# Second attention of a conv-attention network: projections in a written order, values made turned, statistics in PSUM, a scale per slot

## The chip, the cores and the metric

The kernel runs on one core of one Trainium2 chip. It is one launch that computes a whole network of four layers. The metric is the device time of an execution in microseconds (us). Three timed runs of the kernel before gave 3449.45, 3446.09 and 3445.12 us, a median of 3446.09.

The core has engines with instruction queues of their own: TensorE (PE in the profile; PEld is its loading of weights), VectorE (DVE), ScalarE (ACT), GpSimd (POOL) and SyncE (SP). They work side by side and wait for each other by semaphores. SBUF is the memory that all of them read; PSUM is the memory that TensorE writes its products to, in banks of 2 KB for each of 128 partitions.

## The reference, cut to what matters

The input is one image of 256 channels and 64x64 points, so 4096 tokens of width 256. The changed part is the attention of the third layer ("L2"). Its reference, after a layer norm of x and cut to the operations (H = 8 heads of h = 32):

```
q, k, v = linear(x) each, as (B, H, L, h)
sim = sum_d(q * k) * qk_norm_scale
k = l2_normalize(k);  v = l2_normalize(v)
Z = einsum('bhld,bhle->bhlde', v, k) * kv_norm_scale
gates = square(relu(Z.reshape(B, H, L, h*h) @ wg_w.T + wg_b)) + EPS
m_scan, s_scan = online softmax scan of sim along L
Z_scan = cumsum(gates * Z, axis=L);  g_scan = cumsum(gates, axis=L)
softmax_weights = exp(sim - m_scan) / (s_scan + EPS)
attn_weights = Z_scan / (g_scan + EPS) * (1 + silu(softmax_weights))
out = linear(einsum('bhld,bhlde->bhle', q, attn_weights))
```

The result is added to the residual. A mixture of experts follows: layer norm, a router, the two best of eight experts for each token.

## The kernel before, in words

The residual `t` lies in SBUF as 32 tiles of 128 tokens by 256 channels. `attn2` (L1375) goes through it in three stages.

**Projections** (`attn2_project`, L1465; called from L1402). The unit is a block of 4 tiles, 512 tokens; there are 8. For a block, `norm` makes the layer norm (`layer_norm`, in parts by `norm_parts`, L201: statistics on DVE, `root` as an add of eps on DVE, L217, and a square root on ACT, L218, then reciprocal and shift on DVE and the application `a_n` on ACT, L232). `turn` transposes it on PE into channels by tokens (`to_channels`, L238). `project(i)` makes q, k and v of a tile as rows (tokens by channels): two products into PSUM, 512 columns for q and k, 256 for v, and a DVE add of the bias for each (L1492). `turn_v` transposes the values to `vT`. `lengths` squares v and k on ACT (L1499), sums the squares per head on DVE (L1500), multiplies q by k on POOL (L1502) and makes 1/(|v||k|) (L1503 to L1507). `sims` sums the products of q and k (L1511). `gates` mixes `vT` by the gate's weights `wg_bd` on PE, multiplies by k (L1524), sums per head (L1526), and turns the sums into gates (L1527 to L1532), by which POOL multiplies the keys (L1533).

Only PE's order is written by hand here (the loop at L1405 to L1414). The order on DVE, ACT and POOL is made by a scheduler. `to_channels` takes PSUM under the tag "a"; the products of `project` take the tag "b" with four buffers, the mixes the tag "u".

**Factors** (`attn2_fac`, L1560). Sums of the gates and the softmax of sim run along all tokens, so they are scans. The 32 tiles' values are turned so that a partition holds a segment (a segment of 256 tokens of a head), scanned within the segment on DVE, and carried across segments by `carry` (L1592): the segments' ends go through PE to 8 partitions (`a_c`), a short scan runs there, and a second product brings the carry back (`a_back`). This happens twice, for sums and maxima and then for the softmax's total. In between, `beside(n)` issues the next n of 31 state products (`attn2_states`, L1539): the outer products of keys and values of a tile, copied from PSUM by ACT in groups of four tiles (L1554) and summed up along the tiles on POOL (L1556). All four engines' order is written here. At the end stand the reciprocals (L1645, L1648), the Silu (L1647) and the transposed factor, which is copied to `fac` (L1654).

**Sum** (`attn2_sum`, L1656). The unit is a slot `u` of 2 tiles; there are 16. `scale(u)` multiplies q by its factor on POOL (L1671), `bias(u)` adds the output's bias to `t` on POOL (L1674), `turn` transposes q, `scores` makes v times q within the tile and masks it on DVE (L1695), `context` adds what earlier tiles' states give (L1706) to what the tile itself gives (L1712) and scales the sum on ACT (L1725), and `out` projects it (`a_o_ps`) and adds it to `t` (L1731). All four engines' order is written: all scales and biases stand ahead of the loop, and in the loop the router's work of the expert layer (`route`, whose layer norm comes from `norm_parts` too) is woven between the slots.

Of the kernel before, what the change touches and what calls it, by code (L numbers as in the profile page):

```python
# [19 lines left out]
P = 128  # L20
C = 256
# [37 lines left out]
for _name, _n in [  # L59
    ("bout0", 2), ("dw_w", 18), ("dw_b", 2), ("ln_g", 2), ("ln_b", 2), ("b_out", 2), ("bn_g", 2), ("bn_b", 2), ("bn_mean", 2),  # L60
    ("bn_var", 2), ("bq3", 2), ("bk3", 2),
]:
    PP[_name] = slice(_at, _at + _n)
    _at += _n
# [24 lines left out]
class Net:  # L89
# [6 lines left out]
    def constants(self, pool):  # L96
        nc = self.nc
        self.ident = pool.tile([P, P], F32, tag="ident", name="ident")
        make_identity(nc, self.ident)
        self.ones_row = pool.tile([1, P], F32, tag="ones_row", name="ones_row")  # L100
        nc.gpsimd.memset(self.ones_row, 1.0)
        self.one = pool.tile([P, 1], F32, tag="one", name="one")
        nc.gpsimd.memset(self.one, 1.0)
        self.ones_col = self.one

        self.flags = pool.tile([P, 3], F32, tag="flags", name="flags")
        self.mom = pool.tile([P, 2, 2], F32, tag="mom", name="mom")

        self.grp = pool.tile([P, 16, 8], F32, tag="grp", name="grp")
        nc.gpsimd.memset(self.grp, 0.125)  # L110
        nc.gpsimd.affine_select(out=self.grp, in_=self.grp, pattern=[[-8, 16], [0, 8]], base=0,
                                channel_multiplier=1, compare_op=ALU.is_ge, fill=0.0)
        nc.gpsimd.affine_select(out=self.grp, in_=self.grp, pattern=[[8, 16], [0, 8]], base=7,
                                channel_multiplier=-1, compare_op=ALU.is_ge, fill=0.0)
        self.pp = pool.tile([P, NPP], F32, tag="pp", name="pp")
        nc.sync.dma_start(out=self.pp, in_=self.A["pp"])
# [84 lines left out]
    def norm_parts(self, pool, x, out, eps, on_act):  # L201
# [13 lines left out]
        def root():  # L215
            r = got["r"] = room("ln_rstd")
            nc.vector.tensor_scalar_add(r, mv[:, :, 1], eps)  # L217
            nc.scalar.activation(r, r, AF.Sqrt)  # L218
# [1156 lines left out]
    def attn2(self, t, S):  # L1375

        nc, tc = self.nc, self.tc
        with tc.tile_pool(name="a2", bufs=1) as pool:
# [16 lines left out]
            with (  # L1395
                tc.tile_pool(name="a2w", bufs=2) as wp,
                tc.tile_pool(name="a2_ps", bufs=2, space=PSUM) as ps,
            ):
                self.rows(wp, "b_qkv2", "b_qkv2")


                stages = [self.attn2_project(b, t, A, wg_bd, wp, ps) for b in range(NBLK)]  # L1402
                go = lambda b, *names: [stages[b][nm]() for nm in names if 0 <= b < NBLK]
                with tc.manual_schedule(engines={mybir.EngineType.PE}):
                    go(0, "norm", "turn")  # L1405
                    for b in range(-1, NBLK):
                        go(b + 2, "norm")
                        go(b + 1, 0)
                        go(b, "turn_v", "lengths")
                        go(b + 1, 1, 2)  # L1410
                        go(b, "sims")
                        go(b + 1, 3)
                        go(b + 2, "turn")
                        go(b, "gates")  # L1414
# [50 lines left out]
    def attn2_project(self, b, t, A, wg_bd, wp, ps):  # L1465


        nc, w = self.nc, self.w
        tiles = slice(b * TPB, (b + 1) * TPB)
        pairs = slice(2 * b, 2 * b + 2)  # L1470
        heads = lambda x: x.rearrange("p t (h d) -> p t h d", d=D)
        of = lambda nm: A[nm].rearrange("p a s h -> p s a h")[:, pairs]
        by_tile = lambda x: x.rearrange("p (s a) h -> p s a h", a=2)
        q, k, v = A["qk"][:, tiles, 0:C], A["qk"][:, tiles, C:], A["v"][:, tiles, :]
        vT = A["vT"][:, :, b * NB : (b + 1) * NB]
        room = lambda: wp.tile([P, TPB, C], F32, tag="room", name="a2_room", bufs=3)
        held = {}

        def norm():
            held["n"] = wp.tile([P, TPB, C], F32, tag="n", name="a2_n", bufs=1)  # L1480
            self.layer_norm(wp, t[:, tiles, :], held["n"], 1e-5, on_act=True)

        def turn():
            held["nT"] = wp.tile([P, 2, NB], F32, tag="nT", name="a2_nT", bufs=1)
            self.to_channels(ps, "a", held["n"], held["nT"], on_act=True)

        def project(i):
            ti, nT = b * TPB + i, held["nT"]
            for dst, lo, hi in ((A["qk"][:, ti, :], 0, 2 * C), (A["v"][:, ti, :], 2 * C, 3 * C)):
                p = ps.tile([P, hi - lo], F32, tag="b", name="a2_qkv_ps", bufs=4)  # L1490
                self.mm(p, [(nT[:, kt, i * P : (i + 1) * P], w["w_qkv2"][:, kt, lo:hi]) for kt in range(2)])
                nc.vector.tensor_add(dst, p, self.row("b_qkv2")[:, lo:hi])  # L1492

        def lengths():

            ss = wp.tile([P, 2, TPB, NH], F32, tag="ss", name="a2_ss")
            for j, x in ((1, v), (0, k)):
                sq = room()
                nc.scalar.activation(sq, x, AF.Square)  # L1499
                nc.vector.tensor_reduce(ss[:, j], heads(sq), AX.X, ALU.add)  # L1500
            held["tmp"] = room()
            nc.gpsimd.tensor_tensor(held["tmp"], q, k, ALU.mult)  # L1502
            nc.vector.tensor_scalar_max(ss, ss, 1e-24)  # L1503
            nc.scalar.activation(ss, ss, AF.Sqrt)
            held["r"] = wp.tile([P, TPB, NH], F32, tag="r", name="a2_r")
            nc.vector.tensor_mul(held["r"], ss[:, 0], ss[:, 1])
            nc.vector.reciprocal(held["r"], held["r"])  # L1507

        def sims():
            sim = wp.tile([P, TPB, NH], F32, tag="sim", name="a2_simt")  # L1510
            nc.vector.tensor_reduce(sim, heads(held["tmp"]), AX.X, ALU.add)  # L1511
            nc.vector.tensor_tensor(of("sim"), by_tile(sim), bc(bc(self.row("qk_scale"), 1, 2), 1, 2), ALU.mult)

        def turn_v():
            self.to_channels(ps, "a", v, vT, on_act=True)

        def gates():
            u = room()
            for i in range(0, TPB, 2):
                p = ps.tile([P, 2, 2, P], F32, tag="u", name="a2_u_ps")  # L1520
                for j in range(2):
                    for m in range(2):
                        self.mm(p[:, j, m, :], [(vT[:, m, (i + j) * P : (i + j + 1) * P], wg_bd[:, m, :])])
                nc.vector.tensor_mul(u[:, i : i + 2, :], p.rearrange("p t m c -> p t (m c)"), k[:, i : i + 2, :])  # L1524
            g = wp.tile([P, TPB, NH], F32, tag="g", name="a2_g")
            nc.vector.tensor_reduce(g, heads(u), AX.X, ALU.add)  # L1526
            nc.vector.tensor_mul(g, g, held["r"])  # L1527
            nc.vector.tensor_scalar(g, g, self.row("wg_b"), 0.0, ALU.add, ALU.max)
            nc.vector.tensor_mul(g, g, g)
            nc.vector.tensor_scalar_add(g, g, 1e-5)  # L1530
            nc.scalar.copy(of("gate"), by_tile(g))
            nc.vector.tensor_mul(g, g, held["r"])  # L1532
            nc.gpsimd.tensor_tensor(heads(k), heads(k), bc(g, 3, D), ALU.mult)  # L1533

        call = lambda i: lambda: project(i)
        return {"norm": norm, "turn": turn, "lengths": lengths, "sims": sims, "turn_v": turn_v, "gates": gates,
                **{i: call(i) for i in range(TPB)}}

# [21 lines left out]
    def attn2_fac(self, A):  # L1560
# [5 lines left out]
        with (  # L1566
# [25 lines left out]
            def carry(ends, scan, first, fill):  # L1592
# [5 lines left out]
                beside(fill)  # L1598
                self.mm(p.rearrange("p j s -> p (j s)"), [(hot, R.rearrange("p j s -> p (j s)"))])
                c = pool.tile([NH, len(ends), NS], F32, tag="c", name="a2_c")  # L1600
# [6 lines left out]
                beside(1)  # L1607
                self.mm(p, [(hotT, x[:, :, 0:NS])])
                z = pool.tile([P, len(first), NS], F32, tag="z", name="a2_z")
# [10 lines left out]
            def sums_and_tops(x, c):  # L1620
# [16 lines left out]
            nc.vector.tensor_scalar_add(gs, gs, 1e-5)  # L1637
            tot = pool.tile([P, L], F32, tag="tot", name="a2_tot")
# [3 lines left out]
                       (0.0,), 12)  # L1642
# [5 lines left out]
            nc.vector.reciprocal(gs, gs)  # L1648
            nc.vector.scalar_tensor_tensor(s, s, 1.0, gs, ALU.add, ALU.mult)
            beside(len(states))  # L1650
# [5 lines left out]
    def attn2_sum(self, t, A, tri, ked, wp, ps, route):  # L1656
# [15 lines left out]

        def bias(u):
            nc.gpsimd.tensor_tensor(t[:, two(u), :], t[:, two(u), :], bc(self.row("wo_b"), 1, 2), ALU.add)  # L1674
# [66 lines left out]
        with self.tc.manual_schedule(engines={ET.PE, ET.DVE, ET.Activation, ET.Pool}):  # L1741
            scale(0)
            scale(1)
            bias(0)
            turn(0)
            scores(0)
            for u in range(2, U):
                scale(u)
                bias(u - 1)
            bias(U - 1)  # L1750
            for u in range(U + 6):
                if u + 1 < U:
# [1085 lines left out]
def lay_out(i):  # L2838
# [44 lines left out]
        "bq3": cols(i["L3_attn_bq"]), "bk3": cols(i["L3_attn_bk"]),  # L2883
# [30 lines left out]
```

## Time and profile before

| what | us |
|---|---|
| median of three runs | 3446.09 |
| the profiled execution | 3443.01 |
| its span, first to last instruction | 3441.5 |
| projections, first product to `a_rows` | 1445.64 to 1568.44 |
| factors, to the first `scale` | 1568.44 to 1590.69 |
| sum with the router, to about | 1750 |
| PE busy over the span | 3103.2 (90%) |
| DVE, POOL, ACT busy | 2311.1, 1457.5, 1327.2 |

The mean clock that TensorE was granted over the execution was 0.951 of full speed.

How to read the lines of the profile that follow. A line of the timeline gives the start in us from the span's begin, the duration, the engine, the line of the program, the operation, what it writes and reads, the shapes, and a count where several in a row are put together; in brackets stands how long the engine was idle before, and which engine, tile and line ended that wait. A matmul in 32-bit floats is two instructions. A line of the windows gives a stretch, its length, and the busy time and number of instructions of each engine in it, then the granted clock, the busy share of the DMA engines and GB/s.

### The profile page before, as it was taken

The numbers are of one execution on the slowest core, as the hardware profiler recorded it, in microseconds if no ns is written. First come the engines' busy times: TensorE is split into PE (matmuls) and PEld (weight loads), VectorE is DVE, ScalarE is ACT, GpSimd is POOL, SyncE is SP. The second block draws the span as 40 slices with busy tenths as digits, with TensorE's granted clock in tenths as the row PEclk, the third lists the DMA queues.
The fourth block names the chain that finished last, engine by engine and source line by source line (L and its number), as shares of the span: only waits on it lengthen the run. The fifth ranks groups of instructions, "written<-read, shape, count | busy, mean of one in ns | idle before, by whom it ended". The sixth has DMA issues, their size and how long they took to land.

```text
span 3441.5 us, 66218 instructions
## 1 busy us (share of the span) xinstructions
PE 3103.2 (90%) x25772; PEld 2319.7 (67%) x25772; DVE 2311.1 (67%) x5339; ACT 1327.2 (39%) x2554; POOL 1457.5 (42%) x1323
## 2 busy tenths in 40 slices
PE   6779999999977899896969789999999996999997
PEld 3443444344436888665857567888888885999996
DVE  8885777577754677796855576777777775555552
ACT  4444334444425666242633352222222222333331
POOL 2028788778843555326344352000000003555552
PEclk9889999999988999897979899999999997999998
DMA  2146556521134222100158643323333214555554
GB/s 74 40 114 142 161 154 168 130 68 52 48 116 111 68 74 73 44 1 2 52 183 264 215 181 127 98 86 98 99 99 98 91 64 154 200 194 199 206 206 176
DMA packets 241688, 407.01 MB, mean 118 GB/s; under 512 B 78353, under 2 KB 152850, under 8 KB 231890
## 3 DMA queue, kind: packets, MB, share of 16 engines
q1 hardware_dynamic: 212002, 344.40, 32.2%
q0 software_dynamic: 13056, 35.93, 2.8%
q10 hardware_dynamic: 16304, 22.31, 1.9%
q8 instruction: 207, 3.39, 0.4%
q14 instruction: 119, 0.97, 0.1%
HBM read 287.07 MB, written 111.30 MB: 116 GB/s over the span
## 4 chain that ended last, share of the span: by engine, by line
PE 42%; DVE 9%; DMA 5%; issue 5%; ACT 3%; POOL 3%; SPq 0%; POOLq 0%; DVEq 0%; ACTq 0%
PE a_sa_ps L2537 6%; PE f_h_ps L146 5%; DMA ys<-f_y,f_at 3%; PE l_acc_ps L1154 3%; PE a_oa_ps L2576 3%; PE a_ob_ps L2576 3%; PE a_oc_ps L2576 3%; PE a_sb_ps L2537 3%; PE f_ya_ps L146 2%; PE f_yb_ps L146 2%; POOL ys L2292 2%; DVE l_pr L1150 2%; PE a_od_ps L2576 1%; PE a_q_ps L146 1%; PE a_qkv_ps L146 1%
## 5 line engine op out<-in xcount | busy, mean ns | idle before, releaser
L770 ACT COPY l_sc<-l_s 128x384 f32<-128x384 f32 (+1 forms) x632 | 304.0, 532 | 456.9 <-PE l_s L763 445.0
L775 DVE TENSOR_TENSOR l_sm<-l_s,mask 128x256 f32<-128x256 f32 (+2 forms) x628 | 308.2, 552 | 89.2 <-PE l_s L763 88.0
L2103 POOL DMA_INDIRECT xs<-f_room,f_to x64 | 64.5, 1007 | 698.0 <-issue 582.4
L146 PE MATMUL f_h_ps<-f_xT,f_w 128*128 128x256 f32 x1440 | 341.1, 388 | 19.4 <-DVE f_xT L2212 9.7
L146 PEld LDWEIGHTS f_h_ps<-f_xT,f_w 128*128 128x128 f32 x1440 | 262.2, 192 | 84.0 <-ACT f_h L2222 31.3
L763 PE MATMUL l_s<-l_q,l_k 32*128 32x256 f32 (+3 forms) x2944 | 270.5, 453 | 0.0
L2556 ACT ACTIVATE a_e<-a_e 128x512 f32<-128x512 f32 x256 | 156.0, 629 | 246.2 <-DVE a_e L2526 245.2
L780 POOL TENSOR_TENSOR l_sm<-l_sc,mask 128x768 f32<-128x768 f32 (+1 forms) x116 | 201.9, 1748 | 88.2 <-ACT l_sc L770 88.1
L2222 ACT ACTIVATE f_h<-f_h_ps,f_w 128x256 f32<-128x256 f32 x360 | 166.6, 470 | 187.9 <-PE f_h_ps L146 178.7
L1150 DVE TENSOR_TENSOR l_pr<-l_vk,l_w_ps 128x1280 f32<-128x1280 f32 x128 | 186.7, 1482 | 55.2 <-PE l_acc_ps L1154 37.6
L763 PEld LDWEIGHTS l_s<-l_q,l_k 32*128 32x128 f32 x2944 | 132.4, 183 | 115.2 <-issue 67.5
L2292 POOL DMA_INDIRECT ys<-f_y,f_at x144 | 145.7, 1012 | 140.6 <-ACT f_y L2291 110.0
L1154 PE MATMUL l_acc_ps<-ident,l_pr 128*128 128x128 f32 x1600 | 198.1, 278 | 7.7 <-POOL l_pr L1145 7.6
L1154 PEld LDWEIGHTS l_acc_ps<-ident,l_pr 128*128 128x128 f32 x1600 | 184.7, 144 | 14.1 <-POOL l_pr L1145 8.3
L784 POOL TENSOR_TENSOR l_sm<-l_sc,mask 128x256 f32<-128x256 f32 (+1 forms) x220 | 184.9, 868 | 16.1 <-ACT l_sc L770 15.2
L2249 POOL TENSOR_TENSOR f_wt<-f_w 128x512 f32<-128x512 f32 x72 | 89.8, 1268 | 217.1 <-PE f_ya_ps L146 204.9
L2537 PE MATMUL a_sa_ps<-a_q,a_kt 128*128 128x256 f32 x512 | 155.6, 386 | 15.1 <-DVE a_u L2542 14.3
L2541 ACT COPY a_u<-a_sa_ps 128x256 f32<-128x256 f32 x128 | 47.6, 372 | 292.0 <-PE a_sa_ps L2537 292.0
L809 PE MATMUL l_b_ps<-l_sm,l_v 128*32 128x256 f32 (+2 forms) x2176 | 153.7, 372 | 0.0
L2537 PE MATMUL a_sa_ps<-a_qt,a_kt 128*128 128x256 f32 x512 | 152.3, 379 | 0.0
L780 POOL TENSOR_TENSOR l_sm<-l_sc,mask_c 128x768 f32<-128x768 f32 (+1 forms) x64 | 122.9, 1937 | 39.7 <-ACT l_sc L770 39.2
L2537 PE MATMUL a_sb_ps<-a_qt,a_kt 128*128 128x256 f32 x512 | 131.4, 379 | 0.0
(558 smaller groups left out, 7292.1 us busy)
## 6 DMA issues: line engine op xcount, KB each, us to landing
a_kt<-a_kd SPq DMA_DIRECT2D x128, 512.0 KB
f_w<-in_f_w SPq DMA_DIRECT2D x36, 1152.0 KB
f_w<-in_f_w SPq DMA_DIRECT2D x36, 1028.0 KB
xs<-zero SPq DMA_DIRECT2D x8, 4160.0 KB
l_vk<-vt SPq DMA_DIRECT2D x180, 128.0 KB
f_x<-xs SPq DMA_DIRECT2D x72, 260.0 KB
f_w<-in_f_w SPq DMA_DIRECT2D x36, 384.0 KB
l_rcp<-l_recd SPq DMA_DIRECT2D x48, 256.0 KB
```

The source lines that it names most:

```text
L146: self.nc.tensor.matmul(out, lhsT, rhs, start=(i == 0), stop=(i == len(pairs) - 1))
L763: nc.tensor.matmul(s[pair, j][:, at : at + m, :], key(hp), qs[hp], start=(z == 0), stop=(z == len(pieces) - 1))
L770: nc.scalar.copy(sc[:, j], s[1, j])
L775: nc.vector.tensor_tensor(to(pair, j, kind, at), pick(s[pair, j], kind, which), mask, ALU.mult)
L780: nc.gpsimd.tensor_tensor(out[:, :, at, :], of[:, :, which, :], bc(mask, 1, 2), ALU.mult)
L784: nc.gpsimd.tensor_tensor(to(1, j, kind, at), pick(sc[:, j], kind, which), mask, ALU.mult)
L1150: nc.vector.tensor_tensor(pr, vk, bc(held["w"][:, j, dy], 3, D), ALU.mult)
L1154: nc.tensor.matmul(acc[:, m, j, :], pf[:, dx, m * P : (m + 1) * P], self.ident, is_transpose=True, start=(j == 0 and dy == 0 and dx == 0 a ...
L2222: nc.scalar.activation(h[:, m, :], q, AF.Gelu, bias=w1[:, 2 * hidden + m : 2 * hidden + m + 1])
L2292: nc.gpsimd.indirect_dma_start(out=self.ys_parts[(i % 4) * NI + k], in_=y[:, k, :], in_offset=None, out_offset=bass.IndirectOffsetOnAxis(a ...
L2537: mm = lambda out, i, right: nc.tensor.matmul(out, A[i], right, start=True, stop=True)
L2576: nc.tensor.matmul(out, vs[:, j, i, :], right, start=(j == 0 and side != 1), stop=(j == NPAIR - 1 and side != 0))
```

## The change

In `norm_parts`, the root takes eps as the bias of ACT's square root, from a tile `eps` that is made once; the add on DVE goes. This holds wherever `norm_parts` is used.

The projections are one function for all blocks, with the order of PE, DVE, ACT and POOL written out. Values are made turned: the weights stand still and the turned norm moves, in two halves of 128 channels by 512 tokens, and ACT adds the bias while it copies to `vT`. From there PE transposes them back into rows, and ACT copies the rows and squares them, both from PSUM. The squares of the keys go into the room "u" that also holds the mixes' products. Sums per head (`few`) lie in PSUM in a bank of their own. Turns, values and value rows share the PSUM tag "a" with two buffers; the products of q and k have three buffers. The bias of the output is added to `t` here, a block at a time on POOL.

In the factors, the state products stand after the `back` product of each carry and no longer before the two products, 8 after the first and all others after the second. The reciprocal of the gates' sums stands in the second carry, between the product `a_c` and its copy.

In the sum, `scale(u+2)` stands in the loop, one for each slot, and `bias` is gone.

The core of the diff:

```diff
         def root():
             r = got["r"] = room("ln_rstd")
-            nc.vector.tensor_scalar_add(r, mv[:, :, 1], eps)
-            nc.scalar.activation(r, r, AF.Sqrt)
+            assert eps == 1e-5
+            nc.scalar.activation(r, mv[:, :, 1], AF.Sqrt, bias=self.eps[:, 0:1])
...
+        def values(b):
+            h = held[b]
+            for m in range(2):
+                p = ps.tile([P, NB], F32, tag="a", name="a2_v_ps")
+                self.mm(p, [(w["w_qkv2"][:, kt, 2 * C + m * P : 2 * C + (m + 1) * P], h["nT"][:, kt, :]) for kt in range(2)])
+                nc.scalar.activation(vT(b)[:, m, :], p, AF.Identity, bias=self.par("bv2", m))
+
+        def value_rows(b):
+            held[b]["vsq"] = room("sq")
+            for i in range(0, TPB, 2):
+                p = ps.tile([P, 2, C], F32, tag="a", name="a2_vb_ps")
...
+                nc.scalar.copy(v(b)[:, i : i + 2, :], p)
+                nc.scalar.activation(held[b]["vsq"][:, i : i + 2, :], p, AF.Square)
...
+        def squares(b):
+            held[b]["ksq"] = room("u" if b + 1 < NBLK else "n")
+            nc.scalar.activation(held[b]["ksq"], k(b), AF.Square)
...
+        with self.tc.manual_schedule(engines={ET.PE, ET.DVE, ET.Activation, ET.Pool}):
+            for b in range(2):
+                of_block(b)["stats"](range(TPB))
+                held[b]["root"]()
+            norm(0)
+            turn(0)
+            values(0)
+            norm(1)
+            for b in range(NBLK - 1):
+                project(b, (0, 1))
+                across(b, 0)
+                if b > 0:
+                    mixes(b - 1)
+                turn(b + 1)
+                if b + 2 < NBLK:
+                    of_block(b + 2)["stats"](range(2))
+                project(b, (2, 3))
+                across(b, 1)
+                if b > 0:
+                    mixed(b - 1)
+                squares(b)
+                if b > 0:
+                    inverse(b - 1)
+                    gates(b - 1)
+                value_rows(b)
+                values(b + 1)
+                if b + 2 < NBLK:
+                    held[b + 2]["stats"](range(2, TPB))
+                    held[b + 2]["root"]()
+                value_lengths(b)
+                lengths(b)
+                if b + 2 < NBLK:
+                    norm(b + 2)
+                sims(b)
+                bias(b)
...
-            def carry(ends, scan, first, fill):
+            def carry(ends, scan, first, fill, wait=lambda: None):
...
-                beside(fill)
                 self.mm(p.rearrange("p j s -> p (j s)"), [(hot, R.rearrange("p j s -> p (j s)"))])
+                wait()
...
-                beside(1)
                 self.mm(p, [(hotT, x[:, :, 0:NS])])
+                beside(fill)
...
-                       (0.0,), 12)
+                       (0.0,), NT, lambda: nc.vector.reciprocal(upto, gs))
...
-            nc.vector.reciprocal(gs, gs)
-            nc.vector.scalar_tensor_tensor(s, s, 1.0, gs, ALU.add, ALU.mult)
-            beside(len(states))
+            nc.vector.scalar_tensor_tensor(s, s, 1.0, upto, ALU.add, ALU.mult)
...
             scale(0)
+            turn(0)
             scale(1)
-            bias(0)
-            turn(0)
             scores(0)
-            for u in range(2, U):
-                scale(u)
-                bias(u - 1)
-            bias(U - 1)
             for u in range(U + 6):
+                if u + 2 < U:
+                    scale(u + 2)
```

In the diff `across` multiplies q by k on POOL for half a block, `mixes` and `mixed` are the mixing products with their multiply and their sum per head, `value_lengths` and `lengths` the sums of squares with their roots, and `inverse` and `gates` what their names say; `bias` adds `wo_b` to four tiles of `t`. The order of the calls is the order on each engine.

## Prediction

> **What bounds the kernel now.** I looked first at the whole-span summary, then at windows of 14 us through the projections, then at the order of instructions in time in the three stages that the change touches. TensorE (PE) is busy 90% of the span, but that average says little here; the stage decides.
>
> The projections run from 1445.6 us (first `a_qkv_ps`) to 1568.4 (`a_rows`, L1587). The windows (columns: stretch, its length, busy us and count of PE, PEld, DVE, ACT, POOL, then granted clock, DMA share, GB/s):
>
> ```profile
> 1474.00:1488.00 14.00, 14.00 (x66) 9.61 (x65) 13.78 (x29) 6.72 (x15) 4.26 (x2) 1.00 0.00 0
> 1488.00:1502.00 14.00, 13.50 (x64) 9.05 (x63) 13.97 (x26) 5.95 (x12) 4.26 (x2) 1.00 0.00 1
> 1530.00:1544.00 14.00, 14.00 (x66) 9.43 (x65) 13.96 (x24) 6.27 (x12) 4.27 (x2) 1.00 0.00 0
> ```
>
> VectorE (DVE) is as full as PE, but part of that is waiting: in the timeline a 32-column multiply lasts 2 us and ends with a GpSimd (POOL) multiply that began before it.
>
> ```profile
> 1490.76 2.35 POOL L1502 TENSOR_TENSOR a_room<-a_qk 128x1024 f32<-128x1024 f32 x1 [6.61 <-DVE a_g L1526]
> 1491.13 2.03 DVE L1527 TENSOR_TENSOR a_g<-a_g,a_r 128x32 f32<-128x32 f32 x1
> 1494.69 0.18 DVE L1529 TENSOR_TENSOR a_g<-a_g 128x32 f32<-128x32 f32 x1
> ```
>
> So the change has little to win in this stage: PE stands idle at most 0.5 us of 14, and the period of a block is 14.0 to 14.3 us (`a_g` reduces, L1526, at 1474.81, 1489.44, 1503.73, 1517.99).
>
> The sum stage holds the one large hole. In time order:
>
> ```profile
> 1609.08 1.89 PE L146 MATMUL a_o_ps<-w_o,w_qkv 128*128 128x256 f32 x8
> 1613.02 10.62 DVE L217 TENSOR_SCALAR ln_rstd<-ln_mv 128x4 f32<-128x4 f32 x1
> 1623.71 1.28 ACT L218 ACT_TABLE_LOAD   x1 [13.83 <-DVE ln_rstd L217]
> 1625.62 3.78 PE L146 MATMUL a_o_ps<-w_o,w_qkv 128*128 128x256 f32 x8 [10.39 <-ACT w_qkv L1725]
> ```
>
> L217 adds eps to 128x4 numbers, with a median of 165 ns over its 24 calls. Here it takes 10.62 us, exactly as long as POOL runs its scales and biases (L1671, L1674) back to back. ScalarE (ACT) waits for it, PE for ACT: 10.4 us idle. In the chain of waits from 1588 to 1780 it holds 5.5%.
>
> **Projections, after: the sum of a block.** PE's work is the same. Matmuls of 512 columns take 0.43 us an instruction, two to a product. q and k: 16 instructions, 6.88. Values: 8, 3.44 (before they were 256 columns wide, twice as many). Turning the norm and turning the values back: .87 each. Mixes: 16 small ones, 1.79. Sum 13.85 in both. What differs is the order. Written out, PE does: q/k of tiles 0, 1; mixes of b-1; turn of b+1; q/k of tiles 2, 3; value rows of b; values of b+1. Turns, value rows and values share the PSUM tag "a" with two buffers, so the first values matmul needs the first value-rows buffer, which ACT frees after a copy and a Square. On ACT these stand behind `squares(b)`. That writes room "u", which DVE's `mixed(b-1)` must have read; and `mixed` stands on DVE behind the adds of tiles 2 and 3. From the end P of q/k:
>
> - to the last add's start .16 (the PE to DVE hop of the trace), the add .60 (L1492: .55 to .69);
> - the reduce `mixed` 1.16 (L1500, L1526: 1.12 to 1.22) and a hop .03;
> - Square of 1024 columns .95 (L1499: 1.05, .95 from start to start);
> - copy .48 (pairs of L248: 1.07) and Square of half a room .59, hop .05.
>
> That is P+4.05. PE has only .87 of value rows to do: it idles 3.2 us in each of blocks 1 to 6, and 2.1 in block 0, where no `mixed` precedes. Queued behind on PE are values of b+1, then the next q/k: nothing covers it. The period becomes 17.05. The other engines fit: DVE needs some 12 us a block (four adds 2.4, four reduces 4.7, two multiplies 1.3, statistics 1.6, some ten small operations 2), ACT 8, POOL 6.3 (two halves of L1502 2.1, L1533 1.91, the moved bias 2.3).
>
> The POOL waits of DVE (2.03 at L1527, 1.68 at L1506) may go or stay. PE does not notice: they cost .3 of a period before and lie inside the 3.2 after.
>
> Stage: block 0 with values(0) 3.44, its 12.06, 2.1 of stall and the cold start 2.4 (the first 32 instructions took 12.70 instead of 10.3): 20.0. Six blocks of 17.05: 102.3. Block 7 10.2. From the end of its q/k to `a_rows` (before 12.4, with POOL waits in it): two adds 1.2, two multiplies 1.3 (L1524), three reduces 3.5, roots .5, the inverse .5 (L1506, L1507), nine small operations 1.8, hops and DVE's older work 1.0: 9.8. Together 142.3 against 122.8: **+19.4**, of which stalls are 21.3 and the order at the ends gives back 1.9.
>
> **Does a stall cool PE?** Rows: after 2.45 us idle at 1194.22 (1.5 before it) the clock was granted at .57 for 4 us, and l_o_ps x4 took 1.91 where 1.03 is usual; l_acc_ps x10 1.71 against 1.25: 1.35 lost. After 3.19 at 1981.03 and 3.11 at 2093.36 the clock stayed 1.00; after 3.62 at 641.51 it fell.
>
> ```profile
> 1190.00:1194.00 4.00, 1.77 (x16) 1.46 (x14) 2.88 (x5) 3.96 (x6) 0.81 (x1) 1.00 0.00 0
> 1194.00:1198.00 4.00, 3.78 (x15) 3.31 (x16) 1.11 (x2) 3.02 (x6) 2.94 (x3) 0.57 0.51 137
> ...
> 1981.00:1985.00 4.00, 2.82 (x14) 2.21 (x14) 1.38 (x3) 0.96 (x2) 3.76 (x6) 1.00 1.00 373
> ```
>
> Seven stalls by 0 to 1.4: 0 to 10. I take half, **+5**, since the rows split. The Trainium skill ("TensorE: Matmul & The Clock Gate", Part 1) says the clock falls after an idle window of about 3.4 us, a window that runs free: by it a 3.2 us stall would never fill a window, and this term would be 0. The row at 1194 speaks against reading it so strictly.
>
> **Before the first block.** A DVE add (L217) goes, and two statistics blocks of one order take its place: the first `a_n`, 1442.36 now, waits for `wg_bd` (1440.95 at the latest) and not for eight statistics: -1.0 to -2.2, I take **-1.6**. The bias row still comes by ACT's DMA queue, long before the first add. Root without L217 elsewhere (20-odd calls, .17 each, mostly off the path): **-.2**.
>
> **Factors (`attn2_fac`).** I count from E1, the end of the first `back` (1574.70). The state products move behind the `back` matmuls, so ACT's `far` (L1629) comes after two copies of products 0 to 7 (.37 each, with 1.08 of PE work each) and a table load (1.28): the scan L1639 starts at E1+5.5, not 2.98. The reciprocal (1.75, L1648) moves into the gap of the second carry; but that gap, from R to the copy of c, is now some .3 (before, 1.49 because of products in front), so it adds itself to the path: `z` at E1+9.75, not 7.36. Then 23 products, six groups of 1.08 with a copy awaited every second group (about 2.7 us a pair), end with ACT's last copy at E1+17.3. Silu stands behind them all and brings its table load (1.28, now done early at 1579.93 while ACT was idle): 19.0. Then L1649, the transposes and the copy (3.0 to 3.4 now from silu, less POOL): first scale at E1+20.9, not 16.0 (1590.7). **+4.9**; 0 if ACT's copies keep out of its way, +6 at most.
>
> ```profile
> 1579.93 1.28 ACT L1647 ACT_TABLE_LOAD   x1
> 1585.57 0.42 ACT L1647 ACTIVATE a_gs__17338<-a_gs__17338 128x256 f32<-128x256 f32 x1 [4.36 <-DVE a_gs__17338 L1646]
> ```
>
> **Sum stage.** L217 is gone: ACT takes eps as its bias. The biases (16 of 1.09) are in the projections, and scales of 1.05 leave POOL free after six of them, long before the first statistics. So the 10.4 idle goes, and with it the cold matmuls after it (a_o_ps 3.78 against 1.89, a_c_ps 1.55 against 1.08, f_r_ps 1.06 where four turns of that size, a_qT_ps, take .66): 2.8, so 13.2. What is late next is ACT's table load and root (1.5), then the norm that PE turns: 1 to 1.5 back. **-12**; bounds 0 (another narrow DVE operation waits in its place) and -13.2.
>
> **Sum**: -1.6 +19.4 +5 -.2 +4.9 -12 = +15.5. The profiled execution took 3443.0 (span 3441.5): 3458.5. The median of the runs shown, 3446.1, lies 3.1 above it: **3461.6**, slower by .45%. A difference of .2%, 6.9 us, is about what a measurement of this kernel can tell from no change: slower is above 3453.0, faster below 3439.2.
>
> **Rivals.**
> 1. *PE does not wait* (faster): the buffers of tag "a" come free before PE needs them, because `squares` finds room "u" read already or ACT reaches the value rows earlier. For it: only one engine's queue order stands behind my 3.2 us, and DVE would have to be ahead by 3 us; against it: `mixed` cannot start before the adds of q/k, which PE produces right up to P. Then no stall and no cooling: 3461.6-21.3-5 = 3435.3. It decides from a stall of under .6 us a block (3439.2). Chance .10.
> 2. *Half the wait*: `mixed` is not what ACT waits for, only its own queue: stall 2.1 everywhere, no cooling: -6.6 -5 = 3450. Or the factors lose nothing and the clock holds: 3451.7. Within .2%. Chance .16.
> 3. *The hole comes back*: another 128x4 operation (L222, L225) waits for POOL, or out(1) for something as long: 3461.6+12 = 3473.6. For it: two of the three narrow waits in the trace were on operations with two inputs, as L225 has; against it: no POOL work is queued then. Chance .12.
> 4. My sum, 3456.6 (no cooling) to 3466.6 (all stalls cool): .62.
>
> Slower .74 (4 and 3), within .16, faster .10. Leaving out rival 1 and the far half of 3, the range is 3447 to 3474.
>
> **What would show it.** Windows of 17 us in the projections with PE at 13.9 and not 17; a `a_v_ps` row with some 3 us idle before it, released by ACT's Square of the value rows; `squares` released by the reduce `mixed`; clock below 1.00 after it or not. In the factors silu with a table load in front after six copies. In the sum no DVE row above 2 us and `a_o_ps` x8 below 2 us throughout. I am wrong if the blocks repeat every 14 us.

## The result and the profile after

The changed kernel takes 3469.53 us in the median of four runs (3466.29 to 3470.80), the kernel before 3447.39 beside it: a ratio of 1.0063, interval 1.0046 to 1.0080. It is slower by 22 us, where +15.5 was forecast; the time lies inside the range that was given. In what follows PE is warm where its granted clock is 1.00, and cooled where it is half of that.

By stages of the two profiled executions (3441.5 and 3464.6 us of span):

| stage | before | after | difference | forecast |
|---|---|---|---|---|
| start of the first turn (PE `tr_ps`) | 1443.01 | 1438.59 | -4.4 | -1.6 |
| first turn to `a_rows` | 125.43 | 159.09 | +33.7 | +24.4 |
| `a_rows` to the first scale | 22.25 | 28.30 | +6.1 | +4.9 |
| first scale to the end of the last `a_o_ps` | 140.95 | 129.94 | -11.0 | -12 |
| from there to the end | 1709.85 | 1708.66 | -1.2 | - |

Of the 4.4 us at the start, 2.3 lie ahead of the changed part: PE ends layer 1 at 1430.38 instead of 1432.71.

Windows through the projections, in the columns explained above; the period is now 18.6 to 18.9 us, once 20.2, and 17 us hold some 13.9 of PE work, with a granted clock under 1:

```profile
1463.00:1480.00 17.00, 13.90 (x52) 7.92 (x51) 13.20 (x29) 7.03 (x16) 6.40 (x4) 0.86 0.01 1
1480.00:1497.00 17.00, 13.90 (x53) 7.81 (x52) 10.52 (x26) 7.70 (x16) 3.54 (x3) 0.90 0.00 0
1548.00:1565.00 17.00, 13.90 (x52) 7.76 (x51) 11.51 (x24) 7.99 (x16) 6.41 (x4) 0.90 0.00 1
```

The timeline of one wait, over the chain that the prediction named: add, `mixed` (L1551), `squares` (L1509), copy, Square, first values product:

```profile
1492.27 0.69 DVE L1505 TENSOR_TENSOR a_qk<-a_qkv_ps,a_qk_bias 128x512 f32<-128x512 f32 x1 [1.02 <-PE a_qkv_ps L148]
1492.88 1.22 DVE L1551 TENSOR_REDUCE a_few<-a_u 128x32 f32<-128x1024 f32 x1
1494.12 1.06 ACT L1509 ACTIVATE a_u<-a_qk 128x1024 f32<-128x1024 f32 x1 [4.66 <-DVE a_few L1551]
1495.09 0.57 ACT L1498 COPY a_v<-a_vb_ps 128x512 f32<-128x512 f32 x1
1495.55 0.60 ACT L1499 ACTIVATE a_sq<-a_vb_ps 128x512 f32<-128x512 f32 x1
1496.21 5.13 PE L148 MATMUL a_v_ps<-a_nT,w_qkv 128*128 128x512 f32 x8 [3.10 <-ACT a_sq L1499]
```

PE idles 3.10 us, released by ACT's Square, and the eight products after it take 5.13 instead of the 3.70 of a warm block. Windows around this wait show why (the clock is the third number from the end):

```profile
1486.00:1493.00 7.00, 7.00 (x41) 4.90 (x39) 4.59 (x11) 1.20 (x3) 1.27 (x1) 1.00 0.00 0
1496.20:1500.00 3.80, 3.79 (x6) 1.76 (x7) 3.36 (x6) 1.27 (x3) 3.66 (x2) 0.62 0.00 0
```

In this execution each of the seven waits (1.97 in block 0, 3.10 in six) is followed by 3.4 to 6.8 us at half clock. From the busy PE time in those stretches, half of it is lost: 12.5 us.

In the factors, the timeline shows the reciprocal between `a_c` and its copy, and the Silu with its table load behind the last copy of the states:

```profile
1610.22 1.75 DVE L1733 RECIPROCAL a_upto<-a_gs 128x256 f32<-128x256 f32 x1
1610.46 0.26 PE L148 MATMUL a_c<-a_R,a_hot 128*8 128x32 f32 x2 [4.15 <-DVE a_R L1686]
1611.89 0.12 DVE L1691 COPY a_c<-a_c 8x32 f32<-8x32 f32 x1
...
1622.19 0.32 ACT L1644 COPY a_st<-a_st_ps 128x192 f32<-128x192 f32 x1 [0.99 <-PE a_st_ps L1641]
1622.53 1.28 ACT L1738 ACT_TABLE_LOAD   x1
1623.82 0.42 ACT L1738 ACTIVATE a_gs__17293<-a_gs__17293 128x256 f32<-128x256 f32 x1
1624.27 0.43 DVE L1739 SCALAR_TENSOR_TENSOR a_gs__17293<-a_gs__17293,a_upto 128x256 f32<-128x256 f32 x1 [7.89 <-ACT a_gs__17293 L1738]
```

DVE waits 7.89 us for the Silu. In the sum stage the hole is gone: no row of DVE is near 10 us, and the next `a_o_ps` follows at once and warm:

```profile
1649.45 0.30 ACT L220 ACTIVATE ln_rstd<-ln_mv,eps 128x4 f32<-128x4 f32 x1
1649.78 0.18 DVE L224 RECIPROCAL ln_rstd<-ln_rstd 128x4 f32<-128x4 f32 x1 [1.70 <-ACT ln_rstd L220]
1650.24 1.92 PE L148 MATMUL a_o_ps<-w_o,w_qkv 128*128 128x256 f32 x8
```

The sign that `a_o_ps` x8 stays below 2 us throughout did not come: four of its sixteen rows take 2.72 to 3.57 us (before, four took 3.21 to 3.78). Windows around one of them show half clock behind a stretch in which the profile has PE busy all the time:

```profile
1701.50:1714.00 12.50, 12.50 (x231) 11.04 (x228) 9.94 (x26) 8.33 (x15) 6.64 (x8) 1.00 0.19 65
1714.00:1718.00 4.00, 4.00 (x16) 3.11 (x13) 3.56 (x18) 2.56 (x5) 3.23 (x5) 0.57 0.19 67
```

So in this stage half clock comes without a wait of PE too; what brings it there stays open.

### The profile page after: what moved, and what is told of

Its sections match the earlier page's. It is cut to its first block, busy times and chain, and to the rows that moved or that the text cites. A ratio compares the mean times of both kernels' runs of the same rounds, so it can differ in the third digit from the quotient of the medians.

```text
span 3464.6 us, 66062 instructions
## 1 busy us (share of the span) xinstructions
PE 3114.1 (90%) x25708; PEld 2312.7 (67%) x25708; DVE 2287.3 (66%) x5283; ACT 1338.6 (39%) x2578; POOL 1458.2 (42%) x1324
## 4 chain that ended last, share of the span: by engine, by line
PE 44%; DVE 7%; DMA 5%; issue 5%; ACT 3%; POOL 3%; SPq 0%; POOLq 0%; DVEq 0%; ACTq 0%
PE a_sa_ps L2621 6%; PE f_h_ps L148 5%; PE l_acc_ps L1156 3%; PE a_oa_ps L2660 3%; PE a_ob_ps L2660 3%; DMA ys<-f_y,f_at 3%; PE a_oc_ps L2660 3%; PE f_ya_ps L148 3%; PE a_sb_ps L2621 3%; PE f_yb_ps L148 2%; DVE l_pr L1152 1%; PE a_qkv_ps L148 1%; POOL ys L2376 1%; PE a_q_ps L148 1%; PE a_od_ps L2660 1%
```

## The experiments

My theory had four parts: PE waits in each block for a chain over DVE and ACT; the wait cools PE; the factors lose by the order of the state products; the sum stage gains because POOL's row of scales and biases no longer stands where a narrow DVE operation comes. The rivals stand in the expectations. The four sets of runs were made on four chips, and the kernel before took 3494.1, 3494.0, 3447.6 and 3444.5 us in them. So a time is compared only as the ratio to the kernel before of the same set, and stages of the projections and factors by their lengths in the profiles. The sum stage took some 30 to 40 us longer in the profiles of the first two sets (158 to 181 us) than in the others; what makes it so was not looked into.

**The wait, one link at a time.**

```diff
-            held[b]["ksq"] = room("u" if b + 1 < NBLK else "n")
-            nc.scalar.activation(held[b]["ksq"], k(b), AF.Square)
+            if b + 2 >= NBLK:
+                held[b]["ksq"] = room("u" if b + 1 < NBLK else "n")
+            if b + 2 < NBLK:
+                held[b]["ksq"] = vT(NBLK - 1)
+                nc.scalar.activation(vT(NBLK - 1).rearrange("p m (t c) -> p m t c", c=C), k(b).rearrange("p (m t) c -> p m t c", m=2), AF.Square)
...
```

> The squares of the keys of blocks 0 to 5 go into a part of vT that is not written yet, so they need not wait until VectorE has summed the mixes (mixed) out of the room 'u'. Theory (PE's wait is a chain: mixed, squares, copy, Square of the value rows): without mixed in the chain the wait falls from 3.1 to about 2.0 us in blocks 1 to 5, 5.5 us in all, so about 3464; a wait of 1.97 us in block 0 was also followed by half clock, so the cooling should stay; if it goes too, about 3455. Rival (ACT's queue alone delays the value rows, mixed is not what is awaited): the wait stays 3.1, about 3469.

Measured: ratio 1.0029 (1.0016 to 1.0041); 147.2 us from the first turn to `a_rows` instead of 159.1. The wait is 1.97 us in each of blocks 0 to 5, and 3.10 in block 6, which still uses room "u". In the timeline `squares` is now released by the add, not by the reduce:

```profile
1492.57 1.06 ACT L1512 ACTIVATE a_vT<-a_qk 128x1024 f32<-128x1024 f32 x1 [3.52 <-DVE a_qk L1505]
1494.65 2.31 PE L148 MATMUL a_v_ps<-a_nT,w_qkv 128*128 128x512 f32 x3 [1.97 <-ACT a_sq L1499]
```

The 1.1 us that `mixed` was to hold is there. Four of the six waits of 1.97 us were still followed by half clock (6.8 us of it lost); the one of 3.10 was not.

```diff
                 if b > 0:
                     mixed(b - 1)
-                squares(b)
...
                 value_rows(b)
+                squares(b)
                 values(b + 1)
```

> squares(b) is issued after value_rows(b) on ACT and no longer before. Theory: only the copy and the Square of the first value rows are then between PE and its buffer, a wait of about 0.9 us, and at that length no half clock: 13 to 14 us of waits and some 12 us of cooling go, about 3443. If the clock still falls, about 3455. Rival (the order of PSUM buffers only shows the wait; VectorE or ACT sets a period of 17 us): above 3460 with the wait at another tile.

Measured: 0.9970 (0.9956 to 0.9984). The wait falls to 0.74, the period to 14.84, no half clock follows, and the stage takes 130.7 us. The timeline:

```profile
1503.90 2.41 PE L148 MATMUL a_v_ps<-a_nT,w_qkv 128*128 128x512 f32 x5 [0.74 <-ACT a_sq L1499]
```

Its windows:

```profile
1488.00:1491.00 3.00, 2.26 (x8) 1.07 (x7) 2.79 (x10) 2.93 (x5) 1.27 (x1) 1.00 0.00 0
1491.00:1502.00 11.00, 11.00 (x45) 6.30 (x44) 9.40 (x21) 4.97 (x11) 5.15 (x3) 1.00 0.00 0
```

The wait lies in the first stretch, and the clock is 1.00 after it. One call moved by three lines takes 28 us out of this stage (20 against the second profile of the changed kernel, below). So most of the time was lost in ACT's order, and not in the values made turned; 5 us are left against the kernel before.

**An order without this wait meets the next one.**

```diff
-                value_rows(b)
-                values(b + 1)
+                values(b + 1)
+                value_rows(b)
```

> values(b+1) is issued before value_rows(b) on all engines. Theory: the values need only buffers that the turn's copies freed long ago, the value rows then need what vT frees; no wait above 0.5 us, a period near 14, no cooling: 33 us less, about 3436, below the kernel before. Rival (ACT or VectorE is the next bound, since the squares and the value rows now come later in the block): a period of 15.5 to 17, 3447 to 3465.

Measured: 0.9975 (0.9966 to 0.9985), 137.6 us, a period of 15.85 (q and k start at 1480.75 and 1496.60). The rival is right: the wait for buffers is gone, but the turn now trickles behind ACT's norm, and the value rows behind `vT`:

```profile
1486.22 0.33 PE L1481 MATMUL tr_ps<-ident,a_n 128*128 128x128 f32 x1
1486.71 0.33 PE L1481 MATMUL tr_ps<-ident,a_n 128*128 128x128 f32 x1 [0.16 <-ACT a_n L234]
1487.21 0.33 PE L1481 MATMUL tr_ps<-ident,a_n 128*128 128x128 f32 x1 [0.17 <-ACT a_n L234]
```

Between `a_u_ps` and q/k the eight turns take 2.1 us instead of 0.9. None of these waits is long, and after the cold start the clock stays 1.00 in the blocks.

**Does the wait cool PE?** Work in the place of idle time:

```diff
                 p = ps.tile([P, 2, C], F32, tag="a", name="a2_vb_ps")
+                for _ in range(7 * (i > 0 and b + 1 < NBLK)):
+                    nc.tensor.matmul(p.rearrange("p j c -> p (j c)"), self.ident, held[b]["nT"][:, 0, :], start=True, stop=True)
```

> Before the second pair of value rows PE makes seven products of 512 columns that nobody reads (identity times the turned norm, 0.43 us each, 3.0 us), into the same buffer, in blocks 0 to 6: extra work in the place of the idle time. Theory (the wait cools PE, and this costs 12.5 us beside the 20.6 us of the wait itself): no idle time and no half clock there, a period of about 17.0, about 3457. Rival (half clock comes from something else than the idle time, or its cost lies beside other waits): no less than 3467.

Measured: 1.0051 (1.0035 to 1.0068), 166.4 us. The edit was mis-sized: a product of 512 columns is two instructions, 0.86 us, so seven are 6.0 and not 3.0. The clock did stay at 1.00. With three products (the same edit with 3 in the place of 7):

> As the kernel with the extra products, but three of them and not seven: a product of 512 columns is two instructions of 0.43 us, so seven were 6.0 us and these are 2.6, in the place of 3.1 us of idle time. Theory (the idle time cools PE): 0.5 us of idle time left in a block, a period of about 17.0 instead of 18.8, no half clock, about 146 us from the first turn to a_rows instead of 159. Rival: half clock stays, 157 or more.

Measured in one execution: 146.5 us, a period of 17.2, 0.53 idle in a block. Windows:

```profile
1476.00:1493.00 17.00, 16.68 (x62) 9.17 (x62) 13.01 (x30) 7.80 (x17) 6.37 (x4) 1.00 0.00 0
1493.00:1510.00 17.00, 16.63 (x62) 9.17 (x62) 13.00 (x29) 7.79 (x17) 6.42 (x4) 1.00 0.00 1
```

2.6 us of work that nobody reads, in each block, make the stage 12.6 us shorter than in the first profile of the changed kernel, and 4.5 shorter than in the second, in which fewer waits were followed by half clock. So in this stage it is the idle time that cools PE. How often it does differs from one execution to the next, as the changed kernel once more shows:

> The changed kernel itself, on the chip of these runs, to compare the others with. If the ratio of the first comparison holds here: 1.006 to the kernel before. If this chip's longer sum stage gives the shorter row of POOL work more weight than 11 us: 1.003 to 1.005.

Measured: 1.0072 (1.0053 to 1.0091). In its profile the waits are the same (1.97, and six of 3.10 to 3.11), but only three of seven are followed by half clock: 4.9 us lost instead of 12.5, and 151.0 us instead of 159.1. This profile is of the fastest of four executions (3458.71 to 3474.82 us); the two slowest were granted a mean clock of 0.946 and 0.947 and not 0.950, so they probably cooled more often. Its windows show a warm and a cooled block:

```profile
1472.00:1489.00 17.00, 13.89 (x56) 7.87 (x55) 13.12 (x29) 8.00 (x16) 6.42 (x4) 1.00 0.00 0
...
1560.00:1577.00 17.00, 13.22 (x49) 7.30 (x48) 10.39 (x19) 6.73 (x13) 6.41 (x4) 0.90 0.00 0
```

**The factors.** The whole of `attn2_fac` as before:

> The changed kernel with the factors' order of before (state products ahead of the two products of a carry, the second reciprocal at the end). Theory (the new order puts ACT's copies and its table load in front of the exponents and of the Silu): from a_rows to the first scale 22.3 us again and not 28.3, 6 us less. Rival (the new order loses nothing by itself, the later stage of projections delays it): 28 us.

Measured: 1.0028 (1.0010 to 1.0047); 21.8 us from `a_rows` to the first scale instead of 28.3, as the theory had it.

**The sum stage.** The root alone, in the kernel before:

```diff
-            nc.vector.tensor_scalar_add(r, mv[:, :, 1], eps)
-            nc.scalar.activation(r, r, AF.Sqrt)
...
+            nc.scalar.activation(r, mv[:, :, 1], AF.Sqrt, bias=self.eps[:, 0:1])
```

> The kernel before with one part of the change: the root takes eps as the bias of ACT's square root, and VectorE's add L217 is gone; projections, factors, scales and biases as before. Theory (it is L217 itself that stands 10.6 us in POOL's way in the sum stage): the hole before the second router round goes, and 10 to 12 us with it, a ratio to the kernel before of about 0.9970. Rival (the next narrow VectorE operation, the reciprocal L222 or the two-input shift L225, takes its place, since POOL still runs scales and biases back to back): the hole stays, a ratio of 0.9990 to 1.0005.

Measured: 0.9990 (0.9981 to 1.0000). The rival is right. L217 is gone, and the next operation with two inputs takes its place in the timeline, for as long as POOL works without a pause:

```profile
1606.01 0.18 DVE L224 RECIPROCAL ln_rstd<-ln_rstd 128x4 f32<-128x4 f32 x1 [1.70 <-ACT ln_rstd L220]
1606.23 9.04 DVE L227 SCALAR_TENSOR_TENSOR ln_shift<-ln_mv,ln_rstd 128x4 f32<-128x4 f32 x1
1613.09 2.15 POOL L1676 TENSOR_TENSOR t<-t,pr 128x512 f32<-128x512 f32 x2
1616.02 1.46 PE L2053 MATMUL f_r_ps<-ident,a_qk 128*128 128x128 f32 x3 [7.63 <-ACT a_qk L234]
```

The window of L227's wait has POOL (the fifth of the busy times) at work in all of it:

```profile
1606.23:1615.27 9.04, 2.16 (x12) 1.51 (x9) 9.04 (x2) 0.95 (x3) 9.04 (x10) 0.81 0.01 2
```

The opposite part alone, POOL's work by slots with L217 kept:

```diff
             scale(0)
-            scale(1)
-            bias(0)
             turn(0)
+            scale(1)
             scores(0)
-            for u in range(2, U):
-                scale(u)
-                bias(u - 1)
-            bias(U - 1)
             for u in range(U + 6):
+                if u + 2 < U:
+                    scale(u + 2)
+                if u < U:
+                    bias(u)
```

> The kernel before with one part alone: in the sum stage scale(u+2) and bias(u) stand in the loop, one of each in a slot, and not all ahead of it; L217, projections and factors as before. Theory (POOL's long row of scales and biases makes the hole, whichever narrow VectorE operation meets it): no VectorE row above 2.5 us there, no idle time of PE above 3 us before the second slot of the router, a ratio of 0.994 to 0.997. Rival (L217 itself has to go): the 9 to 10 us hole stays, a ratio of 0.999 to 1.001.

Measured: 0.9968 (0.9957 to 0.9980). The stage takes 130.1 us, as in the changed kernel. The group of L217 (minimum, median and longest of 24, in ns) has no long one any more, and the call that took 10.62 us now comes at 1612.63, after POOL had paused for 7.58 us. The longest narrow DVE operation left in the stage is one of the router, of 2.55 us. The group:

```profile
L217 DVE TENSOR_SCALAR ln_rstd<-ln_mv x24: 151/164/273, 1434.9 to 2843.7; 128x4 f32<-128x4 f32 x24
```

**Better versions.** The first moves the value rows ahead, with the factors of before:

```diff
                 project(b, (0, 1))
                 across(b, 0)
+                value_rows(b)
                 if b > 0:
                     mixes(b - 1)
...
+                value_lengths(b)
                 project(b, (2, 3))
...
-                value_rows(b)
                 values(b + 1)
...
-                value_lengths(b)
                 lengths(b)
```

> The changed kernel with the factors of before, and in the projections value_rows(b) after the first half of q and k, ahead of the mixes and the turn, with the sum of the squared values before the second half. Theory (all that the projections lose is the wait for the buffers of tag 'a' and the cooling): no wait above 0.5 us in a block, a period of 13.9 to 14.2, no half clock after the start; from the first turn to a_rows about 126 us, as before, and with the shorter sum stage a ratio to the kernel before of about 0.996. Rival (with the wait gone ACT's norm comes late for the turn, as in values_first): a period of 15 to 16, and a ratio near 1.000.

Measured: 0.9967 (0.9957 to 0.9978), but 135.1 us in the projections and a period of 15.85: the turn waits 1.25 us for a buffer, since ACT's copies of the value rows stand behind a norm that starts late, because DVE's shift takes 1.46 us while POOL adds the bias. The rival is right about the period:

```profile
1489.98 2.00 POOL L1566 TENSOR_TENSOR t<-t,pr 128x1024 f32<-128x1024 f32 x1
1490.53 1.46 DVE L227 SCALAR_TENSOR_TENSOR ln_shift<-ln_mv,ln_rstd 128x4 f32<-128x4 f32 x1
1492.03 2.07 ACT L234 ACTIVATE a_n<-t,ln_shift,ln_rstd 128x256 f32<-128x256 f32 x4 [1.10 <-DVE ln_shift L227]
1495.12 0.66 PE L1481 MATMUL tr_ps<-ident,a_n 128*128 128x128 f32 x4 [1.25 <-ACT a_sq L1499]
```

The second keeps the order of `squares` late, with the factors of before, and frees a buffer after the copy alone:

```diff
                 nc.scalar.copy(v(b)[:, i : i + 2, :], p)
-                nc.scalar.activation(held[b]["vsq"][:, i : i + 2, :], p, AF.Square)
+            nc.scalar.activation(held[b]["vsq"], v(b), AF.Square)
```

> The changed kernel with squares(b) after the value rows on ACT, with the values squared in one piece from their rows in SBUF (so that a buffer of tag 'a' is free after its copy alone), and with the factors of before. Theory: the wait of 0.74 us that squares_late left is a copy and a Square; with the copy alone about 0.2 us stay, a period of 14.3, about 127 us from the first turn to a_rows, 22 us of factors, the short sum stage: a ratio to the kernel before of about 0.994. Rival (ACT is late for the turn, as in values_first and rows_early, since its Square is now one piece of 1.05 us behind the copies): a period of 15 or more and a ratio of 0.996 to 0.998.

Measured: 3427.81 us beside 3447.58, a ratio of 0.9947 (0.9931 to 0.9964). The wait is 0.24, the period 14.34, the projections take 127.8 us, the factors 21.7, the sum stage 128.6. It is faster than both kernels.

```profile
1484.16 3.70 PE L148 MATMUL a_v_ps<-a_nT,w_qkv 128*128 128x512 f32 x8 [0.24 <-ACT a_v L1498]
```

The last one puts only the reciprocal into the gap again, on top of that version:

> As rows_released, with one piece of the changed factors put back: the reciprocal of the gates' sums in the second carry, between the product and its copy, the state products in the order of before. In rows_released that gap is 1.50 us, the reciprocal 1.75, and from the factor's copy (ready at 1586.45) to the first scale POOL is still busy with the states for 1.7 us. Theory (the changed factors lose by the order of the state products; the reciprocal's place matters little): the copy of c comes 0.2 to 0.5 us later, the multiply after the Silu about 1.3 us earlier less that, and the first scale, which waits for POOL, within 0.6 us of 21.7 us after a_rows. Rival (the reciprocal in the gap is what costs the 6 us): 24 us or more.

Measured: 0.9962 (0.9948 to 0.9976), which overlaps the version without it. The first scale comes 21.70 us after `a_rows` instead of 21.74; the factor's transposes come 0.44 us earlier, and POOL, busy with the states, hides that. So the 6 us of the changed factors are not those of the reciprocal by itself, but of the state products' order, perhaps together with the reciprocal in a gap that this order had shortened: the order without the reciprocal was not run.

## Why the prediction was right, and where its sizes were off

**The wait** (3.2 us, 2.1 in block 0): 3.10 and 1.97. Each link was tried: without `mixed` 1.97; without `squares` too 0.74; without the Square 0.24. The estimated period of 17.05 is close to that of the warm blocks (17.2). Without its cooling the stage grew by 20.6 (second profile) to 21 us, where 19.4 was forecast. The first rival, that PE does not wait, is out. Two small slips bear on nothing here: the reduces quoted for the period before lie 14.3 to 14.6 us apart, not 14.0 to 14.3, and 142.3 less 122.8 is 19.5.

**The cooling** (+5, bounds 0 to 10) is the term that was mis-sized in the first profile: 12.5 us, and 4.9 in the second. I priced a stall by 1.4 and took half of them; a cooled stall costs 1.4 to 3.0, and in one execution all seven cooled. The bound of 10 was too low. That the second profile comes to the 5 that was taken is luck: half was a choice between two kinds of rows, and that execution was the fastest of its four. The rule of the Trainium skill that I weighed ("TensorE: Matmul & The Clock Gate", Part 1: a fall after an idle window of about 3.4 us) would have made the term 0. The runs speak against reading it so: waits of 1.97 us were followed by half clock four times in six, in the kernel with `squares` in another room. That section also says that the window runs free of the kernel, and the differing counts of the two profiles of one program agree with that.

**The start** (-1.6): -4.4, of which -2.3 came from ahead of the changed part; -2.1 belong to the step.

**The factors** (+4.9, at most +6): +6.1 and +5.7 in the two profiles. The scan L1639 was forecast at E1+5.5, and came at 5.6; `z` at 9.75, and came at 9.3. The last copy of the states was forecast at E1+17.3 and ended at 18.9: PE stood waiting 1.05 us once within the products, and the groups of products came later than 1.08 and a copy. The Silu stood behind them, as forecast.

**The sum stage** (-12): -11.0 and -12.4 (the second profile has one stretch of half clock less there). The size was right, but the prediction put the removal of L217 first and POOL's free time second. Root alone and POOL by slots alone part them: the first leaves the hole, under L227 (what the third rival named), the second closes it with L217 in place.

Together: -4.4 +33.7 +6.1 -11.0 -1.2 = +23.1 (before rounding) in the profiled executions, against +15.5. The excess is the cooling (7.5), about 2 in the order of the blocks and their ends and 1 each in factors and sum, less 4 in the start and the end, most of it not of the change.

**The range** held in part by luck. The sum's own band ended at 3466.6, with all stalls cooled, and the median of 3469.53 lies above it. The range reached 3474 for the sake of the third rival, a hole that comes back, and no such hole is in the profile. What filled that part of the range is cooling that cost more than its bound.

## What to carry to other kernels

When an order is written out for several engines, follow a shared buffer from its user back through the queue of the engine that frees it: whatever stands ahead of the freeing instruction there, and whatever that waits for, is in the chain. A wait of 2 to 3 us on TensorE can have a second price in the clock, which differs from one execution to the next; measure it by putting work in its place. When a short operation takes 10 us, look at what runs beside it: moving the neighbour helped, removing the operation only passed the wait on.

## What the runs showed of the hardware

A two-input DVE operation of 128x4 waited 9.04 us, not for one POOL instruction of 1.05 to 1.11, but for a row of them without a pause; a one-input reciprocal of the same size (L224) ran in 0.18 beside them. The Trainium skill ("SBUF — State Buffer", "SBUF: two separate sides") says that the pair of ports which both share is held for the whole instruction by whoever comes first, and names two SBUF inputs as one case, a mode of DVE that uses two ports as another. The runs agree on the first, and show that the wait went on from one POOL instruction to the next. L217, which waited 10.62 us, has one input beside its constant; no run here shows in which mode it ran.

TensorE fell to half clock after waits of 1.97 to 3.11 us in three to seven of seven cases, in two executions of the same program (three of seven once more in the run with the factors of before, whose projections are the same), and in none after the waits of 0.24 to 1.25 us that recurred in the blocks of the other versions. This is no full rule for the clock: in the sum stage the granted clock was 0.57 over 4 us that followed 12.50 us without any wait.
